# A quarter of the gated layer among attention's last tiles, shared buffers, and rests fetched at the second square layer

## The chip, the core and the metric

The kernel runs on one core of one Trainium2 chip. The metric is device time in microseconds of one execution. The engines named below are TensorE (PE, its weight loads PEld), VectorE (DVE), ScalarE (ACT), GpSimd (POOL) and SyncE (SP, which here only issues transfers).

## The reference

The input x has shape (2, 2048, 256). It is normalised, and to it are added causal self-attention (one head of width 256) and a gated feed-forward part with ternary weights (-1, 0, 1) and a scale for each output:

```python
xn = _layernorm(x)
out = x + attn(xn, Wq, Wk, Wv, Wo) + ffn(xn, ...)

h = silu(xn @ w1.T * w1_s) * (xn @ w2.T * w2_s)     # gated layer, 256 -> 1024
h = gelu(h @ h1.T * h1_s)                           # first square layer, 1024 -> 1024
h = gelu(h @ h2.T * h2_s)                           # second square layer
return h @ w3.T * w3_s                              # 1024 -> 256
```

All is float32. The kernel splits a float32 operand into a rounded part and the remainder, and multiplies both, with weights that are exact in the rounded form.

## The kernel before

Rows come in 8 tiles of 512 (`n`, four for each of the two sequences). Inside attention a tile is cut into four query tiles `(n, t)` of 128.

**Attention stage.** For a query tile: scores (`score`, L359), exponential and mask on ACT and DVE, then the weights are transposed. Near the diagonal TensorE transposes them (L424, `pt`); the longer ones go "by blocks": DVE turns blocks of 32x32 into a tile `b`, that is stored to DRAM (`d`) and read back transposed into `e`. ACT rounds a block into `pT` (L418), DVE or POOL takes the remainder (L420), and TensorE weighs the values (`weigh`, L438 and L443, `po`). At the end of a tile row, DVE writes `r` (L457) and SP stores it to DRAM as `r_d`. A loop over the tiles interleaves a tile's score steps with an older tile's weighing steps (`merged`, by the costs they are given), and some extra steps listed in the dictionary `extra`. Between those steps the weights are checked for being exact (`beside` takes from the list `looks`), and the factors of h1 are formed; the sums of h1's factors use the memory of `xh0`, in which later the first tile of the normalised input is loaded. A count (`flag`) of entries that need more bits chooses the branch behind attention: `ffn_ternary` when it is zero, `ffn` otherwise. With these inputs it is zero.

**Feed-forward stage, `ffn_ternary`.** Tiles are taken in pairs n, n+1 (n = 0, 2, 4, 6), four passes. A pass:

- `first(n)`: the gated layer, in quarters B11, B12, B22, B21 (the second digit chooses tile n or n+1, that is `xh0` or `xh1`; the first the half of the outputs). A quarter has four outputs of 128; each takes 8 matmuls of 128x512 into two PSUM banks (L736), a Silu on ACT (L741), a multiply on DVE (L742), and for most a split: cast on ACT (L719), remainder on DVE (L720). A split's result goes into the pool `hp`.
- `square` for h1 and h2: a 2x2 block product in seven products instead of eight (Strassen), in the order of `STEPS`: A11, S1, S2, S4, S3, A12, A22 on the weight side, B11, T1, T2, B22, T3, B21, T4 on the other. Each has 32 matmuls (L780), in four PSUM banks, X, Z or Y. Sums on the input side are formed by `t1`, `t2`, `b22` on DVE (L756, L762) and on POOL (L761), and T4 on POOL (L817). Each product's weight factors are loaded by SP from DRAM, 1 MB into one of three buffers (`fetch_factors`, L885).
- `y` for m = n+1, then n: 64 matmuls each (L918), scale (L924), and the rest added (L925), which is the stored attention row `r_d` (L905) plus the rows of x (L907), added on POOL (L908). The rest has one buffer, each y one of three, and each y is stored by SP (L926).

The weight factors of h2 are not in DRAM when this stage starts. In the first pass, `later` gives the places at which they are made: `make_h2(c)` for four parts c loads two rows of h2 (L847), forms four sums on POOL (L151, one buffer `sums`), and stores these (L851); `copy_h2` copies unchanged blocks in DRAM (L860); `load_w3` loads w3 (L855), which POOL rounds (L132). All of these transfers are issued by SP, in program order with the factor loads.

Each engine runs its own instructions in order, and waits for others through semaphores. The order of instructions on an engine is the program's, except where the kernel asks with `issue_after` for an earlier place.

Of the kernel before, what the change touches and what calls it, by code (L numbers as in the profile page):

```python
# [20 lines left out]
P = 128  # L21
# [41 lines left out]
def attn_ffn_kernel(  # L63
# [88 lines left out]

    with ExitStack() as actx:
# [6 lines left out]
        qp = actx.enter_context(tc.tile_pool(name="qp", bufs=2))  # L160
# [4 lines left out]
        ps_s = actx.enter_context(tc.tile_pool(name="ps_s", bufs=4, space=PSUM))  # L165
# [3 lines left out]
        xs, rstds, ks, qs, vs = {}, {}, {}, {}, {}  # L169

# [32 lines left out]
        ps_idle = ps_s.tile([P, TB], F32, tag="ps", name="ps_idle")  # L203
# [8 lines left out]
        def weights_product(name, aT, b, factor):  # L212

            r = cp.tile([P, DC, 2, D], F32R, name=name)
            for c in range(DC):
                ps = ps_s.tile([P, TB], F32, tag="ps", name=f"ps_{name}_{c}")
# [30 lines left out]
        def turn_blocks(src, k, name):  # L247

            b = bp.tile([P, UK * P], F32, tag="b", name=f"b_{name}")[:, : k * P]
            nc.vector.transpose(  # L250
                b.rearrange("p (g k q) -> p k g q", g=P // Q, q=Q),
                src.rearrange("p (k g q) -> p k g q", g=P // Q, q=Q),
            )
            d = dram.tile([P, k * P], F32, name=f"d_{name}")
            nc.sync.dma_start(out=d, in_=b)
            return d
# [51 lines left out]
        def queries(n, m):  # L308
            if m == 0:
                qs[n] = qp.tile([P, DC, 2, TB], F32R, tag="q", name=f"q_{n}")  # L310
            pp = ps_s.tile([P, TB], F32, tag="ps", name=f"pq_{n}_{m}")
# [10 lines left out]
        def values(n, half):  # L322
            if half == 0:
                vs[n] = vp.tile([P, NT, 2, D], F32R, tag="v", name=f"v_{n}")
            pv = ps_s.tile([P, 2, D], F32, tag="ps", name=f"pv_{n}_{half}")
# [18 lines left out]
        def score(n, t, m, order):  # L344
# [10 lines left out]
            ps = ps_s.tile([P, TB], F32, tag="ps", name=f"pss_{n}_{t}_{m}")  # L355
# [73 lines left out]
        def weigh(n, t, m):  # L429
# [12 lines left out]
            for j in range(tiles):  # L442
                nc.tensor.matmul(  # L443
                    out=st["po"][:, 0, :], lhsT=pT[:, 1, ts(j, P)], rhs=vs[m][:, j, 0, :],
                    start=False, stop=(m == n and j == tiles - 1),
                )
# [87 lines left out]

        def store_sums(f, c):
# [13 lines left out]
        def item_factors(src, f, c):  # L549
# [7 lines left out]
            ]  # L557
            items.append(([src[:, c, :], src[:, c + HK, :]], steps))
# [84 lines left out]

        def before(j):
# [18 lines left out]
        while until < len(tiles) - 1:  # L663
# [17 lines left out]
            if not looks and not checked:  # L681
# [3 lines left out]
                pf = ps_s.tile([P, TB], F32, tag="ps", name="pf")  # L685
# [4 lines left out]
        nc.sync.dma_start(out=xh0.bitcast(F32).rearrange("p c h t -> p (c h t)"), in_=xT_d[0])  # L690

    def ffn_ternary(actx):
# [6 lines left out]
        hp = actx.enter_context(tc.tile_pool(name="hpt", bufs=4 * HK))  # L699
        op = actx.enter_context(tc.tile_pool(name="opt", bufs=3))  # L700
        ps = actx.enter_context(tc.tile_pool(name="pst", bufs=8, space=PSUM))

        w3_sb = fw.tile([P, HC, D], F32R, name="w3_sbt")
# [6 lines left out]
        def banks(name, k):  # L710
            return [ps.tile([P, TB], F32, tag="ps", name=f"ps_{name}_{i}") for i in range(k)]
# [4 lines left out]
        def split(f, name):  # L716

            r = hp.tile([P, 2, TB], F32R, tag="h", name=f"h_{name}")
            nc.scalar.copy(r[:, 0, :], f)  # L719
            nc.vector.tensor_tensor(r[:, 1, :], f, r[:, 0, :].bitcast(F32), ALU.subtract)  # L720
            return r

        def first(n):
# [3 lines left out]
            for k in ("B11", "B12", "B22", "B21"):  # L727
                xh = xh1 if k[2] == "2" else xh0
                for i in range(HK):
                    o = i + (HK if k[1] == "2" else 0)  # L730
                    name = f"w_{n}_{k}_{i}"
                    p1, p2 = banks(name, 2)
                    for p, w in ((p1, w1_sb), (p2, w2_sb)):
                        for c in range(DC):
                            for a in range(2):
                                nc.tensor.matmul(  # L736
                                    out=p, lhsT=w[:, c, ts(o, P)], rhs=xh[:, c, a, :],
                                    start=(c == 0 and a == 0), stop=(c == DC - 1 and a == 1),
                                )
                    f = B[k][i] = raw(f"f_{name}")  # L740
                    nc.scalar.activation(f, p1, AF.Silu, scale=sc["w1"][:, o : o + 1])  # L741
                    nc.vector.scalar_tensor_tensor(  # L742
                        f, p2, sc["w2"][:, o : o + 1], f, ALU.mult, ALU.mult
                    )
                    if k == "B11":
                        sets[k].append(split(f, f"{n}_{k}_{i}"))
# [4 lines left out]
                beside(k)  # L751
# [15 lines left out]
        def square(layer, n, B, sets, last):  # L767
# [5 lines left out]
            def product(step, out, start):  # L773
# [11 lines left out]
                if layer == "h1":  # L785
                    beside(step)
# [7 lines left out]
            def summed(k, banks, r):  # L794

                C[k] = r or [raw(f"f_{name}_{k}_{o}") for o in range(HK)]
                for o in range(HK):
# [6 lines left out]
                    if last:  # L804
                        nxt[k].append(split(C[k][o], f"{name}_{k}_{o}"))

            X = banks(f"{name}_X", HK)
            product(0, X, True)
            u1 = kept(X, "u1")
            sets["T3"] = [split(B["B12"][i], f"{name}_T3_{i}") for i in range(HK)]  # L810
            Z = banks(f"{name}_Z", HK)
# [14 lines left out]
            Y = banks(f"{name}_Y", HK)  # L826
            product(5, Y, True)
            summed("B11", Y, u1)
            if not last:
                for i in range(HK):  # L830
                    nxt["B11"].append(split(C["B11"][i], f"{name}_B11_{i}"))
# [11 lines left out]
        def make_h2(c):  # L843
            halves = []
            for k in (c, c + HK):
                t = stgp.tile([P, SC], F32, tag="stg", name=f"stgt_h2_{k}")
                nc.sync.dma_start(out=t, in_=h2[:, k, :])  # L847
# [3 lines left out]
            nc.sync.dma_start(out=factors["h2"][:, 1:5, c, :], in_=sums)  # L851

        def load_w3(c):
            t = stgp.tile([P, SC], F32, tag="stg", name=f"stgt_w3_{c}")
            nc.sync.dma_start(out=t, in_=w3[:, c : c + SC // D, :].rearrange("p c d -> p (c d)"))  # L855
            rounded(w3_sb[:, c : c + SC // D, :].rearrange("p c d -> p (c d)"), t)

        def copy_h2(step):
# [6 lines left out]
            "B11": lambda: make_h2(0), "B12": lambda: copy_h2(0), "B22": lambda: make_h2(1),  # L865
# [4 lines left out]

        def beside(at):
            if at in later:
                later.pop(at)()
# [16 lines left out]

        load_xh(1)
        fetch_factors()

        for n in range(0, N, 2):
# [6 lines left out]
            B, sets = square("h1", n, B, sets, False)  # L901
            B, sets = square("h2", n, B, sets, True)
            for m in (n + 1, n):
                rest = op.tile([P, NT, D], F32, tag="r", name=f"rt_{m}", bufs=1)
# [217 lines left out]
```

## Time and profile before

| | us |
|---|---|
| median of three runs (871.63 to 875.7) | 872.6 |
| the profiled execution | 872.97 |
| its span on the core | 871.1 |
| last matmul of attention ends about | 276.9 |
| first matmul of the feed-forward part | 278.16 |
| first product of h1 starts | 307.56 |
| first product of h2 starts | 360.0 |
| last y matmul ends | 863.96 |
| last DVE addition of the kernel ends | 866.71 |

The profile is of one execution; its time is 0.37 us above the median. The page gives busy time of each engine, the span in 40 slices of 21.8 us, and the chain of work that ended last. A line of the timeline has start, length, engine, line of the kernel, operation, output and inputs, how many instructions were joined, and in square brackets how long the engine had been idle and what released it. A line of the table of waits reads "engine, what it wrote and at which line, what it waited for: total, times, longest". Transfers that SP issues are shown with SPq, and the length is that of issuing, not of the transfer. From 340 us on TensorE has no gaps until the end.

The costliest groups of TensorE work by line, from the page (busy us, mean ns of one, then idle time before it):

```profile
L359 PE MATMUL pss<-k,q 128*128 128x512 f32 (+3 forms) x480 | 110.4, 368 | 2.1 <-DVE q L210 1.1
L438 PE MATMUL po<-v,pT 128*128 128x512 f32 x272 | 79.0, 403 | 3.7 <-ACT pT L418 2.8
L736 PE MATMUL ps_w_B<-xh,w_sb 128*128 128x512 f32 x256 | 59.5, 390 | 1.3 <-DVE r L457 1.3
L780 PE MATMUL ps_h_X<-h_h_T,w_h_S 128*128 128x512 f32 x384 | 89.1, 389 | 0.3 <-DMA w_h_S<-factors_h 0.3
```

The lengths of neighbouring matmuls overlap, so a mean of 390 ns stands for one every 227 ns when TensorE is dense.

### The profile page before, as it was taken

What the parts mean: (1) busy time and instruction counts of PE and PEld (TensorE: products, weight loads), DVE (VectorE), ACT (ScalarE), POOL (GpSimd) and SP (SyncE); (2) the same over time, 40 slices, a digit from 0 to 9 for tenths busy, and PEclk for the clock granted to TensorE, in tenths of its full rate; (3) what the DMA queues carried; (4) which work ended last, traced back from release to release, by engine and by line L of the source; (5) the groups of instructions that cost most, each with busy time, mean ns of one, the idle gap of its engine ahead of it and who ended that gap; (6) DMA issues with size and microseconds to landing.
All of it is one profiled execution on the core that took longest, in us unless ns stands there. A gap on an engine that the chain in (4) does not pass through costs nothing.

```text
span 871.1 us, 12211 instructions
## 1 busy us (share of the span) xinstructions
PE 851.1 (98%) x4280; PEld 720.7 (83%) x4280; DVE 630.3 (72%) x1127; ACT 498.2 (57%) x881; POOL 236.3 (27%) x176
## 2 busy tenths in 40 slices
PE   8999999999989999999999999999999999999996
PEld 5888888988877878888988888988888898888886
DVE  5699688786873995985496596569478648848663
ACT  2547555755644665677266486536657635657670
POOL 4112633201111473540143150025024012402401
PEclk8999999999999999999999999999999999999999
DMA  9867599866792979743424444443444432144412
GB/s 322 312 230 226 176 326 300 298 230 212 243 324 93 375 280 336 273 146 143 139 87 150 146 144 145 149 127 103 145 145 145 146 139 97 49 145 146 145 49 77
DMA packets 63845, 162.51 MB, mean 187 GB/s; under 512 B 6560, under 2 KB 36384, under 8 KB 54560
## 3 DMA queue, kind: packets, MB, share of 16 engines
q1 hardware_dynamic: 58304, 145.92, 48.4%
q10 hardware_dynamic: 5472, 15.73, 5.6%
q8 instruction: 36, 0.59, 0.3%
q14 instruction: 33, 0.27, 0.1%
HBM read 120.21 MB, written 47.71 MB: 193 GB/s over the span
## 4 chain that ended last, share of the span: by engine, by line
PE 61%; DMA 3%; POOL 1%; DVE 1%; issue 0%; SPq 0%; DVEq 0%; POOLq 0%
PE ps_h_X L780 26%; PE ps_h_Z L780 13%; PE ps_w_B L736 10%; PE ps_h_Y L780 7%; PE ps_y L918 6%; DMA stgt_h<-in_ffn_h_w 1%; DMA w_h_S<-factors_h 1%; POOL sums_h L151 1%; DVE f_w_B L762 0%; DMA rt<-r_d 0%; POOL rt L908 0%; DVE h_B L720 0%; DMA out<-yt 0%; POOL f_w_B L761 0%; DVE f_w_B L742 0%
## 5 line engine op out<-in xcount | busy, mean ns | idle before, releaser
L359 PE MATMUL pss<-k,q 128*128 128x512 f32 (+3 forms) x480 | 110.4, 368 | 2.1 <-DVE q L210 1.1
L359 PEld LDWEIGHTS pss<-k,q 128*128 128x128 f32 x480 | 81.6, 189 | 14.9 <-DVE q L210 1.4
L780 PE MATMUL ps_h_X<-h_h_T,w_h_S 128*128 128x512 f32 x384 | 89.1, 389 | 0.3 <-DMA w_h_S<-factors_h 0.3
L780 PEld LDWEIGHTS ps_h_X<-h_h_T,w_h_S 128*128 128x128 f32 x384 | 72.0, 188 | 15.6 <-ACT k_h_u L801 0.7
L438 PE MATMUL po<-v,pT 128*128 128x512 f32 x272 | 79.0, 403 | 3.7 <-ACT pT L418 2.8
L420 POOL TENSOR_TENSOR pT<-e,pT 128x512 fp32r<-128x512 f32 (+3 forms) x30 | 35.6, 1188 | 161.6 <-ACT pT L418 111.0
L908 POOL TENSOR_TENSOR rt<-rt,xt 128x1024 f32<-128x1024 f32 x8 | 19.6, 2453 | 209.9 <-DMA rt<-r_d 209.9
L801 ACT ACTIVATE k_h_u<-k_h_u,h_s_sb 128x512 f32<-128x512 f32 x64 | 46.3, 724 | 41.1 <-DVE k_h_u L800 40.9
L741 ACT ACTIVATE f_w_B<-ps_w_B,w_s_sb 128x512 f32<-128x512 f32 x64 | 43.0, 684 | 43.5 <-PE ps_w_B L736 43.5
L918 PEld LDWEIGHTS ps_y<-w_sbt,h_h_B 128*128 128x128 f32 x512 | 62.0, 192 | 0.3
L918 PE MATMUL ps_y<-w_sbt,h_h_B 128*128 128x256 f32 x512 | 62.1, 283 | 0.0
L736 PE MATMUL ps_w_B<-xh,w_sb 128*128 128x512 f32 x256 | 59.5, 390 | 1.3 <-DVE r L457 1.3
L418 ACT CAST pT<-e 128x512 fp32r<-128x512 f32 (+3 forms) x60 | 32.6, 574 | 48.9 <-DMA e<-d 31.0
L780 PE MATMUL ps_h_X<-h_h_T,w_h_A 128*128 128x512 f32 x256 | 59.3, 389 | 0.0
L780 PE MATMUL ps_h_Y<-h_h_B,w_h_A 128*128 128x512 f32 x256 | 59.3, 389 | 0.0
L736 PE MATMUL ps_w_B<-xh1t,w_sb 128*128 128x512 f32 x256 | 58.7, 389 | 0.0
L438 PEld LDWEIGHTS po<-v,pT 128*128 128x128 f32 x272 | 48.6, 192 | 11.6 <-ACT pT L418 3.3
L736 PEld LDWEIGHTS ps_w_B<-xh,w_sb 128*128 128x128 f32 x256 | 47.8, 188 | 11.2 <-issue 1.5
L780 PEld LDWEIGHTS ps_h_Y<-h_h_B,w_h_A 128*128 128x128 f32 x256 | 48.0, 188 | 10.0
L780 PEld LDWEIGHTS ps_h_X<-h_h_T,w_h_A 128*128 128x128 f32 x256 | 48.0, 188 | 10.0
L736 PEld LDWEIGHTS ps_w_B<-xh1t,w_sb 128*128 128x128 f32 x256 | 48.0, 188 | 10.0
L380 ACT ACTIVATE s<-s,low 128x1024 f32<-128x1024 f32 (+7 forms) x48 | 43.0, 897 | 20.3 <-DVE low L374 19.9
(139 smaller groups left out, 1846.7 us busy)
## 6 DMA issues: line engine op xcount, KB each, us to landing
w_h_S<-factors_h SPq DMA_DIRECT2D x32, 1024.0 KB, 4.7
w_h_A<-factors_h SPq DMA_DIRECT2D x24, 1024.0 KB, 4.7
d<-b SPq DMA_DIRECT2D x18, 512.0 KB, 4.2
e<-d SPq DMA_DIRECT2D x72, 128.0 KB, 4.1
xT_d<-k SPq DMA_DIRECT2D x8, 1024.0 KB, 7.5
stg<-in_ffn_h_w ACTq DMA_DIRECT2D x16, 512.0 KB, 6.6
x<-in_attn_x SPq DMA_DIRECT2D x16, 256.0 KB, 5.5
r_d<-r SPq DMA_DIRECT2D x8, 512.0 KB, 5.3
```

Of the source, the lines that this page charges most:

```text
L151: engine.tensor_tensor(sums[:, i, :], x, y, op)
L359: nc.tensor.matmul(out=ps[:, :w], lhsT=qs[n][:, c, a, ts(t, P)], rhs=ks[m][:, c, b, :w], start=(k == 0), stop=(m < n and k == 3 * DC - 1),)
L380: marks["ACT"] = nc.scalar.activation(st["s"][:, at], st["s"][:, at], AF.Exp, bias=low, accum_out=st["sums"][:, u // UK : u // UK + 1],).ins
L418: nc.scalar.copy(hi, src)
L420: engine.tensor_tensor(lo, src, hi.bitcast(F32), ALU.subtract)
L438: nc.tensor.matmul(out=st["po"], lhsT=pT[:, 0, ts(j, P)], rhs=vs[m][:, j, :, :], start=(m == first and j == 0), stop=False,)
L736: nc.tensor.matmul(out=p, lhsT=w[:, c, ts(o, P)], rhs=xh[:, c, a, :], start=(c == 0 and a == 0), stop=(c == DC - 1 and a == 1),)
L741: nc.scalar.activation(f, p1, AF.Silu, scale=sc["w1"][:, o : o + 1])
L780: nc.tensor.matmul(out=out[o], lhsT=w[:, c, ts(o, P)], rhs=sets[right][c][:, a, :], start=(start and c == 0 and a == 0), stop=(c == HK - 1 ...
L801: nc.scalar.activation(C[k][o], r[o] if r else banks[o], AF.Gelu, scale=s[:, at : at + 1])
L908: nc.gpsimd.tensor_tensor(rest, rest, xt, ALU.add)
L918: nc.tensor.matmul(out=ys[t][:, :D], lhsT=h[c][:, a, ts(t, P)], rhs=w3_sb[:, c, :], start=(c == 0 and a == 0), stop=(c == HC - 1 and a == 1),)
```

## The change

- Four PSUM banks `ps_tiles`, two tiles `q_tiles` and two tiles `b_tiles` are made once and belong to both stages. In attention they are the score banks, the queries and the turned blocks, taken in turn. In the feed-forward stage the `q_tiles` give four places for split operands (`h_views`), the `b_tiles` four places for float32 values (`f_views`), and the banks one of two sets of four; the other set is the stage's own. The pool `hp` has 12 buffers in place of 16.
- The quarter B11 of the first pass is computed inside the attention stage: three of its four outputs as `first_quarter(i)` in `extra` for the last two rounds of the loop; the fourth one's matmuls (`last_quarter`) behind the last weighing matmul, in front of the branch; its Silu and split come at the start of the feed-forward stage. `xh0` is loaded right after the last sums of h1's factors.
- In the first pass the quarters are taken in the order B11, B21, B12, B22. Two of the places in `later` move accordingly.
- `make_h2` and `load_w3` issue their transfers on POOL's queue (`nc.gpsimd.dma_start`), not on SP's.
- The rests of both tiles of a pair are fetched by `rests_of` at the fourth product (step 3) of h2, in the memory of the weight staging tiles; y is added into the rest, which is stored.

```diff
+    q_tiles = [both.tile([P, DC, 2, TB], F32R, name=f"q_{i}") for i in range(2)]
+    b_tiles = [both.tile([P, 2, TB], F32, name=f"b_{i}") for i in range(2)]
+    ps_tiles = [both_ps.tile([P, TB], F32, name=f"ps_{i}") for i in range(4)]
+    h_views = [q_tiles[i // 2][:, i % 2] for i in range(4)]
+    f_views = [b_tiles[i // 2][:, i % 2] for i in range(4)]
...
+        def load_xh0():
+            nc.sync.dma_start(out=xh0.bitcast(F32).rearrange("p c h t -> p (c h t)"), in_=xT_d[0])
...
+            if c == HK - 1:
+                steps.append((0, lambda t: load_xh0()))
...
+        def first_quarter(i):
+
+            banks = [bank(), bank()]
+            gated_products(banks, xh0, i)
+            with tc.issue_after(marks["ACT"]):
+                gated(f_views[i], banks, i)
+                split_into(h_views[i], f_views[i])
+
+        extra[len(tiles)] = [(8 * TB, lambda i=i: first_quarter(i)) for i in range(2)]
+        extra[len(tiles) + 1] = [(8 * TB, lambda: first_quarter(2))]
...
-        nc.sync.dma_start(out=xh0.bitcast(F32).rearrange("p c h t -> p (c h t)"), in_=xT_d[0])
+        last_quarter = [bank(), bank()]
+        with tc.issue_after(marks["PE"]):
+            gated_products(last_quarter, xh0, HK - 1)
...
-        hp = actx.enter_context(tc.tile_pool(name="hpt", bufs=4 * HK))
+        hp = actx.enter_context(tc.tile_pool(name="hpt", bufs=3 * HK))
...
-            for k in ("B11", "B12", "B22", "B21"):
+            for k in ("B11", "B12", "B22", "B21") if n else ("B11", "B21", "B12", "B22"):
...
+                    if n == 0 and k == "B11":
+
+                        if i == HK - 1:
+                            gated(f, last_quarter, o)
+                            split_into(h_views[i], f)
+                        sets[k].append(h_views[i])
+                        continue
...
-                nc.sync.dma_start(out=t, in_=h2[:, k, :])
+                nc.gpsimd.dma_start(out=t, in_=h2[:, k, :])
...
-            nc.sync.dma_start(out=factors["h2"][:, 1:5, c, :], in_=sums)
+            nc.gpsimd.dma_start(out=factors["h2"][:, 1:5, c, :], in_=sums)
...
-            "B11": lambda: make_h2(0), "B12": lambda: copy_h2(0), "B22": lambda: make_h2(1),
+            "B11": lambda: make_h2(0), "B21": lambda: make_h2(1), "B12": lambda: copy_h2(0),
...
+        def rests_of(n):
+
+
+            xt = stgp.tile([P, 2, NT, D], F32, tag="sums", name=f"xt_{n}", bufs=1)
+            rests = {}
+            for m in (n + 1, n):
+                rests[m] = rest = stgp.tile([P, NT, D], F32, tag="stg", name=f"rt_{m}")
+                nc.sync.dma_start(out=rest, in_=r_d[m].rearrange("p (t d) -> p t d", d=D))
+                nc.sync.dma_start(out=xt[:, m - n], in_=rows_of(m))
+                nc.gpsimd.tensor_tensor(rest, rest, xt[:, m - n], ALU.add)
+            return rests
...
-            B, sets = square("h2", n, B, sets, True)
+            B, sets = square("h2", n, B, sets, True, {3: lambda: rests.update(rests_of(n))})
...
-                        nc.vector.tensor_tensor(y, y, rest[:, t, :], ALU.add)
-                        nc.sync.dma_start(out=out[m // NB, rows(m, t), :], in_=y)
+                        nc.vector.tensor_tensor(rest[:, t, :], y, rest[:, t, :], ALU.add)
+                        nc.sync.dma_start(out=out[m // NB, rows(m, t), :], in_=rest[:, t, :])
```

In the changed file the line numbers are higher: make_h2's loads are L915, its stores L919, w3's load L923, the rest's load L962 and its addition L964, POOL's `b22` L826.

## Prediction

> **What bounds the kernel now.** First the page's busy shares and slices:
>
> ```profile
> span 871.1 us, 12211 instructions
> PE 851.1 (98%) x4280; PEld 720.7 (83%) x4280; DVE 630.3 (72%) x1127; ACT 498.2 (57%) x881; POOL 236.3 (27%) x176
> PE   8999999999989999999999999999999999999996
> POOL 4112633201111473540143150025024012402401
> ```
>
> TensorE is nearly always busy; only the start, a slice near 260 us and the end lie below 9. So the work that remains is not cheaper by this change; it can only fill TensorE's gaps. TensorE's table of waits and its timeline tell where they are:
>
> ```profile
> PE po L438 <- ACT pT L418: 2.8, 1, 2.8
> PE ps_w_B L736 <- DVE r L457: 1.3, 1, 1.3
> PE ps_h_Z L780 <- DVE f_w_B L742: 0.5, 1, 0.5
> PE ps_h_X L780 <- DMA w_h_S<-factors_h: 0.3, 1, 0.3
> ...
> 261.04 2.07 PE L438 MATMUL po<-v,pT 128*128 128x512 f32 x4 [2.79 <-ACT pT L418]
> ...
> 278.16 7.52 PE L736 MATMUL ps_w_B<-xh,w_sb 128*128 128x512 f32 x32 [1.28 <-DVE r L457]
> ...
> 307.56 7.55 PE L780 MATMUL ps_h_X<-h_B,w_h_A 128*128 128x512 f32 x32
> ```
>
> Two gaps in attention's last tiles, then the feed-forward part from 278.16. The first gap costs more than its length. The table of stretches (busy PE, weight load, DVE, ACT, POOL; granted clock; DMA share, GB/s) has the clock at 0.66 just after it:
>
> ```profile
> 260.00:265.00 5.00, 3.96 (x15) 3.26 (x15) 2.58 (x5) 3.22 (x7) 1.94 (x2) 0.66 0.42 119
> 265.00:270.00 5.00, 5.00 (x28) 4.34 (x29) 2.71 (x5) 2.47 (x5) 1.39 (x2) 1.00 0.04 15
> ```
>
> Between 261.04 and 264.79 the matmuls come about 0.47 us apart instead of 0.227: some 1.66 us lost. Last, the chain of waits where it matters here, h2's second product of the first pass and the end:
>
> ```profile
> 352.76 14.51 PE ps_h_X L780 x64
> 367.27 7.25 PE ps_h_Z L780 x32
> ...
> 848.61 7.69 PE ps_y L918 x64
> ...
> 857.61 3.33 DMA rt<-r_d
> ...
> 861.11 2.40 POOL rt L908
> ```
>
> and POOL's and SP's timeline for h2's factors:
>
> ```profile
> 333.88 1.30 POOL L151 TENSOR_TENSOR sums_h<-stgt_h 128x512 f32<-128x512 f32 x1 [6.32 <-DMA factors_h<-sums_h]
> 345.74 1.30 POOL L151 TENSOR_TENSOR sums_h<-stgt_h 128x512 f32<-128x512 f32 x1 [6.28 <-DMA factors_h<-sums_h]
> 351.06 0.37 SPq L851 DMA_DIRECT2D factors_h<-sums_h  x1
> 360.34 7.28 SPq L885 DMA_DIRECT2D w_h_S<-factors_h  x3
> ```
>
> A round of sums has one buffer, so it waits 6.3 us for the last store. The last store is issued at 351.06, its factors are asked for at 360.34 and wanted at 367.27. This row of rounds is what an earlier start of the feed-forward part runs into.
>
> **What the Trainium skill says.** "DMA: Bandwidth & Descriptors", section "Anatomy of one DMA — SWDGE (gpsimd) path", gives about 2.0 us plus bytes/436e3 for a transfer issued by POOL, and its Specifications some 1 us to the first byte against 0.6 from SP. No POOL-issued transfer is in this trace; SP's 1 MB stores take 6.1 us here, well above the 4.4 that formula gives[...]. "SBUF — State Buffer", in "SBUF: two separate sides", warns that descriptors written by POOL are held up while VectorE holds the port shared with it (a transfer of 620 ns became 3100). The trace shows the sharing for arithmetic: L720 takes 0.69 us alone and 1.1 to 1.8 beside POOL's adds. "TensorE: Matmul & The Clock Gate", Part 1, puts the half clock after an idle window of some 3.4 us; here 2.79 us of waiting already brought 0.66.
>
> **The change part by part**, against the profiled execution: 872.97 us, span 871.1; the median is 872.6, so 0.37 lower.
>
> 1. Attention's end. A quarter of the gated layer is 32 matmuls of 0.227 = 7.26 us. In the built order 24 of them (5.45 us) stand among the last tiles, 11 after the po of tile t=0, the others before the transposes and in the po of t=1; 8 (1.8 us) follow the last po, before the branch. The 2.79 and the 1.66 behind the first gap are filled and the 1.28 is too, 5.7 in all. So the first matmul after the branch comes at about 279.7 with one quarter already done, where before the quarter ended at 285.4: 5.7 us gained. ACT's Silu (0.69), its casts (0.6) and a table load (1.28, seen at 279.39 before) fall in ACT's idle 258.45 to 260.37; if not, PE waits up to 1 us. SP's order at the end of attention stays; the load of xh0 was at 241.68 already. The banks split in four shared and four own come free in time by the order of products: 0.
>
> 2. First pass. Before, from 278.16 to 367.27 are 89.11 us, for 4 x 7.26 + 8 x 7.25 = 87.04 of work: 2.07 us of waits. After, three quarters and eight products from 279.7 end at 279.7 + 21.8 + 58.0 = 359.5. DVE is full from 290 to 325 and lags by 0 to 2 us at h1's third product; this is covered by the next item.
>
> 3. h2's factors now go over POOL's own queue: loads L915, stores L919, w3's loads. Each is an instruction on POOL, with whatever is queued behind it. The order after the second round's sums is: load, store, load, round, load, store, load, three sums, an add (L826), the fourth sum, a w3 load, an add, the last store. Six issues lie on the path. Say t is the cost of one: below by SP's 0.33, so nearly nothing; above by 2 us, the fixed cost of the page, or more if VectorE locks POOL out. I take 0.5, between SP's 0.33 and the page's 1 us to first byte. The second round ended at 327.56 before. A rest's add (2.84, at 309.23) leaves POOL there, and VectorE's quarter B21 comes earlier, against the start of B22 1.5 us later: I put it at 324.5. Two stores (6.3 each) and two rounds (5.3 each) are 23.2, two adds of 1.72 are 3.4, together 26.6. Last store: 324.5 + 26.6 + 6 x 0.5 = 354.1. Landing 6.1, SP's turn 0.2, S1's load 5.0 (median 5.9 with three at once): S1 is there at 362.4 + 6t = 365.4. Also on SP, S1 stands behind the rest's load (L962), which waits for the rounding of w3's first half and its freed slot: load issued near 351, 7.0 us, round 1.2, so about 360, no later. So PE waits at h2's second product from 359.5 to 365.4, only 1.9 us earlier than before, and such a wait costs the clock too: I take 1.7 us, as after 2.79 us above (0.7 to 3.4). Net gain up to there: 0.2 us. What attention gave is mostly handed back here. Later passes don't build factors; they stay dense.
>
> 4. The end. Before, after the last y matmul at 863.96 came: the late rest (single buffer), 2.40 us of POOL, and out of three y buffers, to 866.71: 2.75 us. After, both rests are fetched at h2's fourth product and lie ready; multiply and add (0.42 + 0.43) remain, 0.92. Gain 1.83. In the passes before, POOL's two adds fall where VectorE has slack; 0, at most 1 us.
>
> 5. Attention's early tiles: the fixed bank and block buffers reorder some waits at 0 to 30 and 100 to 240 us (7.5 us of idle there, all told); nothing says which way. 0, within 2.
>
> Sum: 0.2 + 1.8 = 2.0. 872.97 - 2.0 = **871.0**.
>
> **Rivals.**
> - The factors come in time. It needs t near zero and the second round ended by about 322.5 with shorter landings, S1 there by 360.5. For it: SP is freed of waiting stores (one of those had held the factors of h1 that cost 0.28 at 337.99). Then 367.27 - 359.5 = 7.8 and 1.8, less up to 2 of DVE's lag: 872.97 - 8.6 = 864.4. Chance 0.15.
> - They come a little late: round ended at 322.5, t 0.3, S1 at 362.2. 5.1 gained, 1.7 of clock, 1.8 at the end: 867.8 (866 to 869). Chance 0.27.
> - Slower: POOL's descriptors are starved by VectorE. At t = 2.0 S1 is there at 374.4: 7.1 later than before, 1.7 of clock, less 1.8: 880.0. It decides from t = 1.6, where the loss passes 4.4 us. For: VectorE runs almost without a gap on SBUF operands. Against: its tensor_tensor here slowed, and was not stopped, beside POOL. Chance 0.18.
> - That attention's gap is not filled (the quarter itself waiting for xh0 or ACT) would cost nothing more in the forecast, as the wait for S1 absorbs it.
>
> **How the numbers follow.** The forecast, S1 at 364 to 370, 869.5 to 875.5, has 0.40. Telling apart from no change needs about 0.5%, 4.4 us. Faster than 868.2: the in-time case and nearly all of the next (0.25), 0.40; slower than 877: 0.18; the rest 0.42. The likeliest case alone is 869 to 876; for 8 in 10 the range must reach into both neighbours: 863.5 leaves out some 0.05 below, 878.0 some 0.14 above.
>
> **What would show it.** Item 1: the two waits at 258 and 277 gone, clock 1.00 in 260 to 265, the first quarter after the branch at 279.7. Item 3: a wait of 5 to 6 us of ps_h_ on w_h_S at the second product of h2, first pass only, and a lowered clock after it; the last sums' end near 353, S1's issue near 360. Item 4: 0.9 us from the last y matmul to the last add. It is wrong if no such wait stands there (then 864), if the wait is above 12 us (then slower), or if another pass is no longer 145.9 us.

## The result and the profile after

| | before | after |
|---|---|---|
| median of 6 runs | 874.47 us (871.63 to 875.95) | 882.28 us (881.01 to 884.59) |
| profiled execution, time / span | 872.97 / 871.1 | 883.71 / 881.8 |
| idle TensorE before 257 us | 7.9 | 11.5 |
| TensorE asks for h2's second product | 367.1 | 363.6 |
| that product begins | 367.1 | 377.15 |
| last store of h2's factors issued | 351.06 | 364.96 |
| last y matmul to last addition | 2.75 | 0.90 |

The changed kernel takes 1.0102 times as long, interval 1.0082 to 1.0123. The forecast was 871.0, no change; it is slower. The profiled executions lie 1.5 us below and 1.4 us above their medians, so their difference, 10.7 us, is larger than the 7.8 between the medians. First the page of the kernel after:

```profile
span 881.8 us, 12244 instructions
PE 851.1 (97%) x4280; PEld 720.4 (82%) x4280; DVE 645.6 (73%) x1127; ACT 499.6 (57%) x881; POOL 234.2 (27%) x190
...
PE   8999989999999999489999999999999999999997
...
POOL 4012643101211574750133042024215002502300
PEclk9999999999999999889999999999999999999999
```

TensorE's busy time is the same 851.1 us. The 8 of the slice that ends at 261 us is now a 9, and a new hole stands in the seventeenth slice, 353 to 375 us: a 4, with a lower clock there and in the next. The sixth slice, 110 to 132 us, has gone from 9 to 8: that is a loss in the middle of attention, to which item 1 below comes back. TensorE's table of waits (line, what it waited for: sum, times, longest) and its timeline after show it:

```profile
PE ps L846 <- DMA w_h_S<-factors_h: 13.5, 1, 13.5
...
281.43 3.83 PE L170 MATMUL ps<-xh,w_sb 128*128 128x512 f32 x16
...
356.19 7.41 PE L846 MATMUL ps_own<-q,w_h_A 128*128 128x512 f32 x32
377.15 9.57 PE L846 MATMUL ps<-h_h_T,w_h_S 128*128 128x512 f32 x32 [13.54 <-DMA w_h_S<-factors_h]
386.56 7.42 PE L846 MATMUL ps_own<-h_h_T,w_h_S 128*128 128x512 f32 x32
```

One wait of 13.5 us, at the place where the forecast had one of 5.9. S1 is the name of the factors that this product, h2's second, was waiting for. The product lasts 386.56 - 377.15 = 9.4 instead of 7.25 us. The table of stretches of after (length; busy PE, weight load, DVE, ACT, POOL; clock; DMA share, GB/s) says why, and that attention's gap is filled:

```profile
260.00:265.00 5.00, 5.00 (x29) 4.28 (x28) 2.29 (x6) 4.97 (x9) 0.00 (x0) 1.00 0.90 284
...
370.00:375.00 5.00, 0.00 (x0) 0.00 (x0) 5.00 (x8) 3.91 (x8) 2.12 (x2) 0.50 1.01 378
375.00:380.00 5.00, 2.85 (x7) 2.27 (x8) 5.00 (x4) 1.47 (x3) 5.00 (x4) 0.50 1.01 393
```

At 260 to 265 there are 29 matmuls instead of 15, clock 1.00. At 375 to 380 the clock is 0.50, and 2.2 us are lost on top of the wait. What TensorE waited for is made on POOL. POOL's timeline after, from the last subtractions of h1 to the last store of h2's factors:

```profile
317.29 1.68 POOL L885 TENSOR_TENSOR f_w_B<-f_w_B,f_w_B 128x512 f32<-128x512 f32 x1 [0.63 <-DVE h_T L184]
320.80 3.39 POOL L885 TENSOR_TENSOR f_w_B<-f_w_B,f_w_B 128x512 f32<-128x512 f32 x2 [1.83 <-DVE h_T L184]
324.15 1.73 POOL L151 TENSOR_TENSOR sums_h<-stgt_h 128x512 f32<-128x512 f32 x1
...
330.94 0.57 POOL L915 DMA_DIRECT2D stgt_h<-in_ffn_h_w  x1
331.51 0.77 POOL L919 DMA_DIRECT2D factors_h<-sums_h  x1
332.27 0.53 POOL L915 DMA_DIRECT2D stgt_h<-in_ffn_h_w  x1
340.76 1.28 POOL L151 TENSOR_TENSOR sums_h<-stgt_h 128x512 f32<-128x512 f32 x1 [7.96 <-DMA factors_h<-sums_h]
343.46 1.30 POOL L151 TENSOR_TENSOR sums_h<-stgt_h,stgt_h 128x512 f32<-128x512 f32 x1 [1.43 <-DMA stgt_h<-in_ffn_h_w]
...
355.60 1.73 POOL L151 TENSOR_TENSOR sums_h<-stgt_h 128x512 f32<-128x512 f32 x1 [5.86 <-DMA factors_h<-sums_h]
...
364.96 0.80 POOL L919 DMA_DIRECT2D factors_h<-sums_h  x1
```

and in the kernel before, the end of the second round and the issue of its store:

```profile
325.94 1.62 POOL L151 TENSOR_TENSOR sums_h<-stgt_h,sums_h 128x512 f32<-128x512 f32 x1
...
327.58 0.37 SPq L851 DMA_DIRECT2D factors_h<-sums_h  x1
```

Three things are to be seen. The second round of sums begins only when all four subtractions L885 are through (before, one sum stood ahead of the fourth), and these wait for VectorE's splits: the round ends at 330.94, 3.4 us later than before, though h1's first product had begun 2.5 earlier (305.05 against 307.56). The third round comes 9.25 us after the store's issue (before: 333.88 - 327.58 = 6.3), and then waits 1.43 us for its second load (before: 0.25). Every transfer stands on POOL itself: 0.53 to 0.57 us for a load, 0.77 to 0.81 for a store. Last, the chain of waits of after, in this stretch and at the kernel's end:

```profile
332.27 11.13 DMA stgt_h<-in_ffn_h_w
...
348.44 7.01 DMA factors_h<-sums_h
...
364.96 5.65 DMA factors_h<-sums_h
...
370.73 6.38 DMA w_h_S<-factors_h
...
876.20 0.43 DVE yt L997
...
876.65 0.42 DVE rt L998
```

The difference between the two profiled executions is settled at this one point: TensorE begins the product after it at 386.7, before at 374.5, so 12.2 us later; from there to the last y matmul both kernels take 489.4 us. The end gives 1.85 back, and its last store takes 0.3 longer: 10.7 us, the difference of the spans.

### The profile page after: what moved, and what is told of

Its sections match the earlier page's. It is cut to its first block, busy times and chain, and to the rows that moved or that the text cites. A ratio compares the mean times of both kernels' runs of the same rounds, so it can differ in the third digit from the quotient of the medians.

```text
span 881.8 us, 12244 instructions
## 1 busy us (share of the span) xinstructions
PE 851.1 (97%) x4280; PEld 720.4 (82%) x4280; DVE 645.6 (73%) x1127; ACT 499.6 (57%) x881; POOL 234.2 (27%) x190
## 4 chain that ended last, share of the span: by engine, by line
PE 75%; DMA 10%; POOL 4%; DVE 4%; issue 4%; ACT 1%; SPq 1%; ACTq 0%; POOLq 0%; DVEq 0%
PE ps L846 20%; PE ps_own L846 20%; PE ps L170 7%; PE ps L399 6%; PE ps_own L170 6%; PE po L478 4%; DMA e<-d 3%; PE ps_own L991 3%; PE ps L991 3%; POOL sums_h L151 2%; PE po L483 2%; PE ps L371 2%; DMA d<-b 1%; DMA factors_h<-sums_h 1%; DMA stgt_h<-in_ffn_h_w 1%
## 5 line engine op out<-in xcount | busy, mean ns | idle before, releaser
L399 PE MATMUL ps<-k,q 128*128 128x512 f32 (+3 forms) x480 | 109.0, 366 | 2.5 <-DVE s L408 1.7
L399 PEld LDWEIGHTS ps<-k,q 128*128 128x128 f32 x480 | 81.5, 189 | 15.0 <-DVE s L408 2.1
L964 POOL TENSOR_TENSOR rt<-rt,xt 128x1024 f32<-128x1024 f32 x8 | 20.0, 2497 | 166.7 <-DMA rt<-r_d 62.2
L478 PEld LDWEIGHTS po<-v,pT 128*128 128x128 f32 x272 | 47.5, 189 | 13.5 <-issue 2.7
L826 POOL TENSOR_TENSOR k_h_u<-k_h_p,k_h_u 128x512 f32<-128x512 f32 x16 | 22.5, 1407 | 116.1 <-ACT q L183 102.5
L408 DVE TENSOR_SCALAR_CACHE_REDUCE s<-ps 128x512 f32<-128x512 f32 (+3 forms) x80 | 47.1, 599 | 3.7 <-PE ps L399 3.1
L483 PEld LDWEIGHTS po<-v,pT 128*128 128x128 f32 x272 | 42.5, 189 | 6.2 <-DVE pT L460 0.5
L483 PE MATMUL po<-v,pT 128*128 128x256 f32 x272 | 46.1, 283 | 0.0
L846 PE MATMUL ps<-h_h_T,w_h_S 128*128 128x512 f32 x128 | 31.8, 409 | 13.5 <-DMA w_h_S<-factors_h 13.5
L184 DVE TENSOR_TENSOR q<-k_h_u,q 128x512 fp32r<-128x512 f32 x32 | 44.2, 1411 | 0.1
L290 DVE STREAM_TRANSPOSE b<-s 128x1024 f32<-128x1024 f32 (+3 forms) x30 | 33.6, 1127 | 8.8 <-ACT s L420 7.7
L885 POOL TENSOR_TENSOR k_h_p<-f_h_B,k_h_p 128x512 f32<-128x512 f32 x16 | 32.5, 2061 | 16.3 <-DVE h_h_T L184 16.3
L170 PE MATMUL ps<-xh,w_sb 128*128 128x512 f32 x144 | 35.8, 391 | 0.0
L826 POOL TENSOR_TENSOR f_w_B<-f_w_B,f_w_B 128x512 f32<-128x512 f32 x16 | 25.7, 1620 | 37.5 <-DVE f_w_B L179 37.4
```

The lines of the kernel that those rows point to most:

```text
L170: nc.tensor.matmul(out=p, lhsT=w[:, c, ts(o, P)], rhs=xh[:, c, a, :], start=(c == 0 and a == 0), stop=(c == DC - 1 and a == 1),)
L399: nc.tensor.matmul(out=ps[:, :w], lhsT=qs[n][:, c, a, ts(t, P)], rhs=ks[m][:, c, b, :w], start=(k == 0), stop=(m < n and k == 3 * DC - 1),)
L408: marks["DVE"] = nc.vector.tensor_scalar(st["s"][:, ds(at, w)], ps[:, :w], 1.0, None, ALU.mult, ALU.max, accum_out=st["tops"][:, m - first ...
L478: nc.tensor.matmul(out=st["po"], lhsT=pT[:, 0, ts(j, P)], rhs=vs[m][:, j, :, :], start=(m == first and j == 0), stop=False,)
L483: marks["PE"] = nc.tensor.matmul(out=st["po"][:, 0, :], lhsT=pT[:, 1, ts(j, P)], rhs=vs[m][:, j, 0, :], start=False, stop=(m == n and j == ...
L826: nc.gpsimd.tensor_tensor(B["B12"][i], B["B22"][i], B["B12"][i], ALU.subtract)
```

## The experiments

Three causes stood against each other: the rounds on POOL (their place in POOL's order, and one buffer of sums); the queue, that is the transfers issued by POOL; and attention, whose tiles are now used in a fixed turn. Ratios are to the kernel before, run beside on the same chip, 95% interval in brackets.

**e1_sp**: the changed kernel with the three kinds of transfer on SP again.

```diff
-                nc.gpsimd.dma_start(out=t, in_=h2[:, k, :])
+                nc.sync.dma_start(out=t, in_=h2[:, k, :])
...
```

> The changed kernel, with the transfers of h2's factors and of w3 issued by SP again as before; all else as changed. If POOL's queue is what makes the factors late (each issue takes 0.5 to 0.8 us of POOL, and stores and loads stand behind POOL's additions), the wait for S1 at h2's second product falls from 13.5 us to under 5 and the time to about 870 to 873. If instead the rounds are late because the second one starts late (at 324, behind POOL's T4 subtractions, which VectorE releases), the queue matters little: a wait of 10 us or more stays and the time is 878 to 882.

Measured: 879.71, ratio 1.0066 [1.0041, 1.0091], some 3 us better than after, with intervals that overlap. TensorE's and POOL's timeline of e1_sp:

```profile
375.00 9.46 PE L846 MATMUL ps<-h_h_T,w_h_S 128*128 128x512 f32 x32 [7.28 <-DMA w_h_S<-factors_h]
...
341.04 1.29 POOL L151 TENSOR_TENSOR sums_h<-stgt_h 128x512 f32<-128x512 f32 x1 [9.15 <-DMA factors_h<-sums_h]
...
355.75 1.86 POOL L151 TENSOR_TENSOR sums_h<-stgt_h 128x512 f32<-128x512 f32 x1 [9.44 <-DMA factors_h<-sums_h]
```

The wait is 6.3 us shorter, but the product begins only 2.15 earlier: in this run TensorE itself came later, at 367.7. The rounds come at the same times, since each still waits over 9 us for a store. So moving the transfers back is not enough in the changed kernel, and a slow landing of the stores is not a matter of POOL's queue alone. The wait neither went away nor stayed, so this run alone does not decide between the causes.

**e4_noneed**: h2's first pass reads h1's factors, which are there early; the rounds run as in the changed kernel.

```diff
-                    in_=factors[layer][:, step].rearrange("p c o -> p (c o)"),
+                    in_=factors["h1" if n == 0 else layer][:, step].rearrange("p c o -> p (c o)"),
```

> The changed kernel, where the first pass of h2 multiplies by h1's factors, which are long in DRAM, in place of h2's, so nothing waits for the rounds of sums (these are still made). If the wait for S1 and the lower clock after it are the whole loss, 13.5 + 2.2 = 15.7 us go: about 866.6. If other waits stand right behind it (the next factors, VectorE's splits, the rests), less than 10 us go: above 872.

Measured: 874.57 (20 runs), 1.0006 [0.9991, 1.0021]. The wait for the factors is gone, and with it the loss, but nothing is gained on before. TensorE's waits in e4_noneed:

```profile
PE ps_own L846 <- DVE h_h_T L184: 4.0, 4, 1.8
```

Here h2's third product takes from 371.31, the end of the second, to 385.90: 14.6 us instead of 7.25, of which 4.0 are waits, with a clock of 0.50 at 375 to 380. The splits it waits for need POOL's additions L826, for which VectorE waits 3.9 us, and these stand in POOL's order behind and between the fourth round's sums. So the rounds hold up two things, the factors and h2's own operands.

**e9_norounds**: the changed kernel with h1's factors for all of h2, no round of sums and no copies of h2's blocks.

```diff
...
-            0: lambda: copy_h2(5), 1: lambda: make_h2(2), 2: lambda: copy_h2(6),
-            3: lambda: make_h2(3), 5: lambda: load_w3(0), 6: lambda: load_w3(SC // D),
+            5: lambda: load_w3(0), 6: lambda: load_w3(SC // D),
...
```

> The changed kernel without h2's factors: make_h2 and copy_h2 are left out, and all products of h2 use h1's factors. What stays is the filled end of attention, the fixed buffers (measured at +4.2 alone) and the earlier rests. If POOL's rounds and the wait for their result are all that is wrong behind attention, this is 873.3 + 4.2 - 5.7 (gaps filled) - 2.0 (first pass's small waits) - 1.8 (end) = 868.0, and TensorE has no wait over 1 us from 283 us on. If VectorE's load in the first pass is a bound of its own, waits of VectorE's splits stay and it is above 872.

Measured: 870.6 (20 runs), 0.9956 [0.9942, 0.997]. Against after's ratio that is 1.5%, some 13 us, that hang on making h2's factors: the loss and more. It also shows what the rest of the change gives: 3.8 us, not the 8.6 of the rival "in time". TensorE's waits and timeline of e9_norounds:

```profile
PE ps L846 <- DVE h_T L184: 2.4, 2, 2.1
...
365.36 7.42 PE L846 MATMUL ps<-h_h_T,w_h_S 128*128 128x512 f32 x32
```

h2's second product begins at 365.4 without a wait; ahead of it, at h1's third product, TensorE waits 2.4 us for VectorE's splits h_T.

**e8_chain**: the changed kernel with another order on POOL only: the subtractions L885 of h1's first pass behind the third round's store, h1's output additions behind the last store.

```diff
...
-                nc.gpsimd.tensor_tensor(t4, B["B21"][i], t4, ALU.subtract)
+                with after_round(2) if (layer, n) == ("h1", 0) else nullcontext():
+                    nc.gpsimd.tensor_tensor(t4, B["B21"][i], t4, ALU.subtract)
...
```

> The changed kernel, with POOL's order alone changed: T4's four subtractions of the first pass of h1 stand behind the third round's store, and the four additions for h1's output behind the last store, so that the rounds go first. If the order on POOL makes the rounds late, S1 lands 11 to 14 us earlier, the wait falls to 0 to 3 us and the time to 867 to 870. If the transfers themselves are what is slow, the wait stays above 8 us: 876 or more.

Measured: 876.35, 1.0039 [1.002, 1.0058]: 5.5 us better than after. TensorE's waits in e8_chain:

```profile
PE ps L847 <- DVE h_h_T L184: 3.5, 2, 2.5
PE ps_own L847 <- DVE q L184: 2.9, 2, 2.1
```

The last store goes out at 356.30 instead of 364.96, and the wait for factors is gone altogether, as was expected of POOL's order; the time is not, because what was moved behind the rounds is now late itself. POOL's order decides who waits. It does not remove the waits while the rounds begin 13 to 17 us apart (317.64, 334.85, 348.13).

**e12_both**: as e8, with two buffers of sums (paid for by four blocks of the raw pool, 25 to 21), the subtractions behind the third round's loads, and the first pass's rests behind the last factor load.

```diff
...
-            sums = stgp.tile([P, 4, HB], F32, tag="sums", name=f"sums_h2_{c}", bufs=1)
+            sums = stgp.tile([P, 4, HB], F32, tag="sums", name=f"sums_h2_{c}", bufs=2)
...
```

> The changed kernel with a second buffer for the rounds' sums (raw buffers 21 in place of 25 give the memory), T4's subtractions of the first pass behind the third round's loads, h1's four output additions behind the last store, and the first pass's rests fetched behind the factor loads on SP. If one buffer and POOL's order make the rounds late, S1 lands before 364, no wait over 2 us stays in the first pass, and the time is 867 to 870. If the rounds are held by their transfers whatever the order, S1 is still 6 us or more late: 875 or more.

Measured: 877.47 (20 runs), 1.0043 [1.0029, 1.0057]; no better than e8, and TensorE waits 9.1 us for S1 again. No round waits for a store now, but POOL's timeline of e12_both has another wait in that place:

```profile
305.75 0.54 POOL L919 DMA_DIRECT2D stgt_h<-in_ffn_h_w  x1
...
321.37 1.30 POOL L151 TENSOR_TENSOR sums_h<-stgt_h,stgt_h 128x512 f32<-128x512 f32 x1 [6.65 <-DMA stgt_h<-in_ffn_h_w]
...
340.38 1.29 POOL L151 TENSOR_TENSOR sums_h<-stgt_h,stgt_h 128x512 f32<-128x512 f32 x1 [5.47 <-DMA stgt_h<-in_ffn_h_w]
```

The second load of a round is issued just behind the 1 MB store on the same queue, at 305.75; the sum that reads it starts at 321.37, 15.6 us later.

**e13_sp**: e12 with these transfers on SP, and the moved work behind the rounds' third sums rather than behind POOL's issues.

```diff
...
-                fetched[c] = nc.gpsimd.dma_start(out=t, in_=h2[:, k, :]).ins
+                nc.sync.dma_start(out=t, in_=h2[:, k, :])
...
```

> As e12_both (two buffers for the sums, the rounds ahead of T4 and of h1's output additions on POOL, the first pass's rests behind the factor loads), but with h2's and w3's transfers issued by SP as before. If the serial order of POOL's transfers is what held e12's rounds (a load issued behind a store took 15 us), S1 lands before TensorE asks for it, no wait over 2 us is left in the first pass, and the time is that of e9 without rounds, 869 to 872, below before. If the rounds are bound by POOL's additions and VectorE, or SP's queue holds them as long, a wait of 5 us or more stays: 876 or more.

Measured: 869.83, 0.9939 [0.9917, 0.9961]: the first version faster than before. TensorE's, POOL's and SP's timeline of e13_sp:

```profile
365.58 7.42 PE L850 MATMUL ps<-h_h_T,w_h_S 128*128 128x512 f32 x32
...
346.78 1.30 POOL L151 TENSOR_TENSOR sums_h<-stgt_h,stgt_h 128x512 f32<-128x512 f32 x1 [8.90 <-DMA stgt_h<-in_ffn_h_w]
...
351.17 0.37 SPq L926 DMA_DIRECT2D factors_h<-sums_h  x1
```

The last store is at 351.17 against 358.46 in e12, and h2's second product waits for nothing. Yet the fourth round still waits 8.9 us for a load issued behind a store, now on SP's queue; the rounds are early enough to bear it. From e12 to e13 the queue, with the points behind which the work is moved, is worth some 9 us by the ratios; the two were not told apart. From after to e1 the queue was worth 3: there each round waits over 9 us for its store on SP's queue too.

**e11_queue**: the reverse, the queue alone: before, with the three kinds of transfer on POOL.

```diff
-                nc.sync.dma_start(out=t, in_=h2[:, k, :])
+                nc.gpsimd.dma_start(out=t, in_=h2[:, k, :])
...
```

> The kernel before, with the transfers of h2's factors and of w3 issued by POOL, and nothing else. If POOL's issues of 0.5 to 0.8 us are the queue's whole cost, S1 lands 3 to 5 us later than before, of which some 1.5 were slack: 2 to 4 us lost, 875 to 877. If POOL's queue is no slower than SP's, whose loads stand behind each other, nothing is lost: 872 to 874.5.

Measured: 882.66, 1.0088 [1.0056, 1.0121]. By itself the queue costs the kernel before about as much as the whole change costs, and more than was expected. TensorE's and POOL's timeline of e11_queue:

```profile
371.32 9.85 PE L780 MATMUL ps_h_Z<-h_h_T,w_h_S 128*128 128x512 f32 x32 [4.77 <-DMA w_h_S<-factors_h]
...
338.72 1.29 POOL L151 TENSOR_TENSOR sums_h<-stgt_h,stgt_h 128x512 f32<-128x512 f32 x1 [2.18 <-DMA stgt_h<-in_ffn_h_w]
...
359.60 0.77 POOL L851 DMA_DIRECT2D factors_h<-sums_h  x1
```

The last store is issued 8.5 us later than before (351.06). The third and fourth rounds bring 2.2 and 2.1 of it in waits for the load that stands behind the store, and each round has three issues on POOL (0.57 + 0.77 + 0.54 = 1.9 us), the last of which runs beside the store's landing. The wait of 4.8 us then costs 2.4 us of clock.

**e2_tail**: before, with only the rests fetched early, as in the change (in the first pass behind the last factor load).

```diff
-                rest = op.tile([P, NT, D], F32, tag="r", name=f"rt_{m}", bufs=1)
+                rest = rests[m]
...
+                elif step == (3 if n else 5):
+                    with nullcontext() if n else tc.issue_after(loads[-1]):
+                        rests.update(rests_of(n))
```

> The kernel before, with the rests of a pair fetched at the fourth product of h2 into the staging tiles and y added into them, as in the change (in the first pass behind the factor loads, so that they don't stand ahead of S1). If only the end counts, 1.8 us are gained: 871.5. If the earlier transfers or POOL's additions disturb the passes, nothing is: 873 or more.

Measured: 876.77 (20 runs), 1.0032 [1.0017, 1.0047], no gain but a small loss. The end does shrink, with the last y matmul at 873.09 and the last addition at 873.59 to 874.0. But in e2_tail's profile the product at 352.29 waits 3.8 us for another load of h2's factors (w_h_A) and lasts 9.0 us. What on SP made that load late is open. The profiled execution is the slowest of the 20, 4.1 us over their median, and its attention, which the edit leaves alone, ends 4.1 us later than in before's; so how much of the median's loss this wait explains is not shown.

**e3_fixed, e15_banks, e16_blocks**: before, with attention's tiles in a fixed turn: all three kinds (score banks, queries, blocks), the banks alone, the blocks alone. The queries alone were not tried. The edit of the banks:

```diff
...
-        ps_s = actx.enter_context(tc.tile_pool(name="ps_s", bufs=4, space=PSUM))
+        ps_s = actx.enter_context(tc.tile_pool(name="ps_s", bufs=1, space=PSUM))
+        ps_tiles = [ps_s.tile([P, TB], F32, name=f"ps_{i}") for i in range(4)]
...
```

> The kernel before, with attention's score banks, queries and turned blocks as fixed tiles taken in turn, as in the changed kernel, and nothing else. If these make attention's middle slower (idle TensorE before 257 us 11.5 in the changed kernel, 7.9 before), about 3.7 us are lost: 878. If that loss comes from the quarter, the earlier load of xh0 or chance, it stays at the time of before, within 1.5 us.

> The kernel before, with only attention's four score banks as fixed tiles taken in turn. If the banks are the part of the fixed buffers that costs (e3: +4.2 with banks, queries and blocks fixed), 877 to 878; if the blocks are, or both together, 873 to 875.

> The kernel before, with only the two turned-block tiles fixed. If the blocks are the part that costs, 877 to 878; if the banks are, 873 to 875. If both runs lose about as much, it is not the one buffer but any change of the order in which attention is laid out that costs.

Measured: 877.52, 1.0052 [1.0037, 1.0068]; 887.47, 1.0131 [1.0096, 1.0167]; 873.26, 0.9981 [0.9963, 0.9999]. The blocks cost nothing; the banks do, and alone far more than the 877 to 878 expected. The stretches of e15_banks, and of before beside it:

```profile
150.00:200.00 50.00, 46.58 (x272) 41.09 (x271) 39.33 (x111) 28.74 (x61) 7.12 (x7) 0.97 0.78 248
200.00:250.00 50.00, 47.47 (x244) 39.55 (x243) 32.54 (x83) 24.74 (x51) 8.45 (x6) 0.97 0.60 179
```

```profile
150.00:200.00 50.00, 50.00 (x301) 44.62 (x300) 40.65 (x116) 30.26 (x66) 7.36 (x6) 1.00 0.80 265
200.00:250.00 50.00, 49.10 (x261) 42.01 (x260) 42.15 (x101) 30.03 (x58) 10.26 (x7) 1.00 0.77 251
```

With banks in a fixed turn TensorE is busy 5 us less in these 100 us and its clock falls from 1.00 to 0.97. The whole loss of that profile lies in attention: the first matmul behind it comes at 293.33 instead of 278.16. But by the medians the same edit costs 13 us alone and 4 with the two others, so this is no fixed price of the banks. That it goes through the order in which attention is laid out is likely, and not shown.

**e17_pool**: e13, with attention's banks from a pool again and all four outputs of the first quarter finished inside attention.

```diff
...
-        extra[len(tiles) + 1] = [(8 * TB, lambda: first_quarter(2))]
+        extra[len(tiles) + 1] = [(8 * TB, lambda i=i: first_quarter(i)) for i in (2, 3)]
...
```

> As e13_sp, but attention's score banks come from a pool again, as before the change, and all four outputs of the quarter are finished inside attention, so that no bank is shared across the branch (queries and blocks stay shared). If the fixed banks are what disturbs attention (e15: banks alone +13, e16: blocks alone -1), attention ends some 4 us earlier, against 1.3 us of waiting for banks behind the branch: 866 to 868. If any new layout of attention costs about as much, it is 870 or more.

Measured: 865.1, 0.9907 [0.9883, 0.993], the fastest of all. The product is on time here too, and the page of e17_pool has no slice below 9 between the first and the last:

```profile
span 867.6 us, 12266 instructions
...
PE   8999999999999999999999999999999999999997
```

## Why the prediction was wrong

**Item 1, attention's end.** The mechanism was right: gap filled, clock 1.00. The place in time was not. The last eight matmuls of the quarter were to begin at 279.7 - 1.8 = 277.9 and began at 281.43, 3.5 late. TensorE idles 11.5 us before 257 us instead of 7.9. That is item 5, put at "0, within 2": with e3 it is 4.2 us. One profile can't show it, for executions of the same attention differ as much: in the seven profiles that have the changed one (after, e1, e4, e8, e9, e12, e13) these matmuls begin between 277.74 (e8) and 282.41 (e1), on average at 280.7. So 3.5 is what this execution shows, 2.8 the average, and 4.2 what e3's 13 runs show.

**Item 2.** TensorE asked for h2's second product at 363.6, not 359.5; 3.5 of the 4.1 are attention's. Where all rounds are gone or on time, it begins at 365.4 (e9), 365.6 (e13) and 365.3 (e17), not at 359.5. In e9 2.9 of these 5.9 us are attention's and 2.4 the wait for VectorE's h_T at h1's third product, which item 2 named as a lag of 0 to 2 and left to item 3 to cover. So the rival "in time" did not have 7.8 us to win in any of these profiles, but some 1.8.

**Item 3 is the step that failed**, and in it above all one term, the end of the second round. The wait was put at the right place and behind the right chain, but S1 was there at 377.15, not 365.4, so 11.75 us late, and the wait of 13.5 us passed the 12 that the forecast had itself named as a sign of being wrong. Of the 11.75 us, 10.9 are in the last store's issue (364.96 against 354.1):
- The second round ended at 330.94, not 324.5: 6.4 us, the largest term. I took an earlier VectorE and an absent rest's addition off before's 327.56. In fact the stage began 3.5 later, three issues now lie on POOL ahead of the subtractions (0.57 + 0.81 + 0.54 = 1.9 us), and VectorE was not earlier: POOL waits 2.50 + 1.23 + 0.63 + 1.83 = 6.2 us for it between 309.6 and 320.8, before 4.4. From 285 to 295 us VectorE is busy 5.6 us, before 9.3, as B11's splits are nearly all done by then and the quarter B21, which is now the second, gives it none; from 295 to 335 it is full. That this order of the quarters is what made the splits late was tried by no run. Nor were the subtractions the only gate: in e8, which moves them, the second round begins at 317.64, after 7.66 us of waiting for the first round's store.
- From that end to the third round 9.8 us, where the sum had 7.3 (a landing of 6.3 and two issues): 2.5.
- The third round took 7.1 instead of 5.3, as it waited 1.43 for its own load, which stood behind the store. No term of the sum had this.
- t, the disputed cost of an issue, was nearly right: 0.53 to 0.57 for loads, 0.77 to 0.81 for stores, taken as 0.5. The six on the path took 4.0 us, and the sum had 3.0.

The last store's landing was put at 6.1. Before, the four stores took 11.5, 6.1, 6.1 and 9.2 us from issue to landing, so 6.1 was that of the middle two; that the last one took 5.7 after, and the term did no harm, is luck. The load of S1 took 6.4 instead of 5.0. The clock cost 2.2 instead of 1.7.

The rival "slower" gave 880.0 with S1 at 374.4, and its outcome came, but its reason did not: POOL's issues were not starved, the three at 330.94 to 332.80 took 0.57, 0.77 and 0.53 us, with VectorE busy 5.00 of 5.00 us at 330 to 335. So the warning that the forecast took from the Trainium skill, "SBUF — State Buffer", section "SBUF: two separate sides", was not borne out here: that page measured it beside a copy on VectorE, and what ran on VectorE beside these three issues were the splits, of the form tensor_tensor. That S1 came about as late as in that rival (377.15 against 374.4) is luck. The lateness came from the end of the second round and from slower landings. What slows the landings is not shown; with the transfers on SP's queue, in e1, the two stores took 9.0 and 9.3 us. A loss from these causes was missing in my cases: the bounds stood on t alone, while the second round's end had no upper bound.

**Item 4** was right: 0.90 us from the last y matmul to the last addition, 1.85 gained; the passes after the first are still 145.9 us apart. That early rests cost nothing is not borne out: e2 is 0.3% slower than before, where 1.8 us were to be gained.

What stays open: how the loss is shared between POOL's order, its one buffer and its queue, which act on each other (the queue is worth 8 us in e11, 3 in e1 and, with other points of order, 9 in e13); why banks in a fixed turn cost 4 or 13 us by what else changes; whether e17 is faster than e13 at all (0.3%, intervals that overlap), and how a gain would be shared between its two edits.

## What to carry to other kernels

A gap filled early in the kernel pays only as far as the next chain of producers has slack: work out when that chain can end from its own gates, here VectorE's splits, POOL's order, the one buffer and the landing of each transfer, and bound each of them, before counting the gain. Transfers moved to the queue of an engine that also computes stand in line with its arithmetic, 0.5 to 0.8 us each here. A load issued behind a large store is late on either queue, so it may pay to issue it ahead; a second buffer for sums that are stored helped in e13, together with another order and queue, and not in e12. Neither was tried by itself. Sharing memory between two stages can also cost the earlier stage, 4.2 us in e3; try that part alone.

## What had not been expected of the hardware

- What a load of 512 KB takes from issue to landing depends on whether it stands ahead of a round's 1 MB store or behind it. In the second and third rounds, ahead of the store: 3.5 and 4.8 us on SP's queue (before), 3.9 and 3.8 (e13), 4.9 and 4.5 on POOL's (after). Behind it: 7.3 and 6.9 (before), 9.2 and 9.1 (e13), 11.1 and 7.5 (after). In the first round, with the DMA engines busy all the time (a share of 1.0 at 300 to 310 us), those behind took 12.4 us (before), 15.7 (after) and 15.6 (e12). In these runs the place matters more than the queue.
- Waits of 3.8 us (e2) and 4.8 (e11) cost a further 1.7 and 2.4 us of clock, as much as one of 13.5 (2.2): the product behind each is stretched from 7.25 to 9.0, 9.7 and 9.4 us. A wait of 2.4 us in e13 cost 1.8, with a clock of 0.81 and 0.85 in the stretches from 320 to 330; one of 2.15 in e9 cost 0.2, with a clock of 1.00.
- The same attention differs in length by 4 us and more between profiled executions: by 4.7 from e8 to e1 for the changed one, and by 4.3 from e11 to e2 for the one before, where the first matmul behind it comes at 277.93 and 282.24.
